# Four transfers made one, DRAM scratch laid out anew, and a reordered step in a delta-rule attention and ternary FFN kernel

## The chip, the cores and the metric

The kernel runs on one core of a Trainium2 chip. The metric is device time in microseconds (us) of one execution; lower is better. A profile comes from one execution of its own, and its span (first to last instruction) is a little shorter than that execution's time. The engines are PE (matrix multiply; PEld is its weight load), DVE (vector), ACT (scalar, activations), POOL (GpSimd) and SP, which here only issues DMA transfers.

## What is computed

Input x has 4 sequences of 4096 tokens of width 512, in float32. Two layers follow each other, each with a layer norm in front, one behind, and a residual.

```python
x = x + layernorm(attn(layernorm(x)))      # attn: a delta rule over time
x = x + layernorm(ffn(layernorm(x)))       # ffn: a ternary 512 x 512 weight

# attn, 16 heads of 32: rk = x normalised per head, wk = rk one step earlier,
# v = x @ Wv.T, gate and beta = sigmoid(x @ Wg.T), sigmoid(x @ Wb.T); per time step:
pred = einsum('bhk,bhkd->bhd', wk_t, S)
S    = S + wk_t[..., None] * ((v_t - pred) * b_t)[..., None, :]
o    = einsum('bhk,bhkd->bhd', rk_t, S) * g_t
# attn's result: o @ Wo.T

# ffn: layer norm with ln_gamma, ln_beta; w_q = clip(round(weight / (beta + EPS)), -1, 1)
# with beta = mean|weight|; xq = clip(xn * 128 / gamma) with gamma = max|xn| over everything;
# y = (xq @ w_q) * (gamma * beta / 128)
```

## The kernel before

Time is cut into 128 units of 32 tokens. A unit is 32 tokens of all four sequences, so its tiles have 128 partitions: partition `32*b + t` holds token t of sequence b. Within a unit the recurrence is solved as a block: a 32 x 32 triangular matrix per sequence and head is built, inverted, and applied to the right-hand side; only the small state S goes from one unit to the next.

Two strands of work run in one loop of steps.

- The strand of the blocks, at unit k ("AHEAD" in the plan): `load` brings x, `x_stats` and `x_norm` make its layer norm (DVE, then four small POOL instructions), `keys`, `keys_turn`, `key_squares`, `key_sums` and `key_norms` make the keys, `values` and `values_rest` multiply by Wv, `grams` multiplies keys by keys, `blocks` (ACT) and `masked` (POOL) turn that into the triangular blocks `nat`, which go to DRAM (`nat_d`). `hT` and `v` go to DRAM too (`hT_d`, `v_d`). `values` also makes `gr`, the gate moved by one token: two small transfers inside SBUF, one of 127 partitions (L248) and one of 4 partitions (L249); the second writes the same tile and waits on SP's queue until the first has landed.
- The inverses. `gather` reads `nat_d` back in another order, so that a partition holds one sequence and head (4 sequences x 32 heads of two units = 128) with a whole 32 x 32 block. `invert` works on groups of up to 8 units (DVE, `pr` L348 and `na` L354), a share of it at each place where the plan has a number such as 0.35. The inverses go to DRAM (`q_d`), and `fetch_inverse` reads them back with a token per partition.
- The strand of the chain, at unit i ("BACK"): `fetch` brings v and hT back, `again` brings x a second time for the residual, then `predict`, `apply`, `errors`, `outputs` and `grow` (the recurrence), `out_turn`, `project`, `residual` (with x1 to DRAM), `x1_stats`, `x1_norm`, `x1_turn`, `x1_scale`, `largest` (xn to DRAM), `ternary_a`, `ternary_b` and `finish`, which stores y.

Every transfer but a handful is issued by SP, in the order of the program. Each of `load`, `again`, `finish`, `gather` and `fetch_inverse` issues four transfers, one for each sequence b, with 32 partitions each.

The order of work on each engine is the order in which the functions are called: each instruction is tied to the one before it on its engine. The tuple `plan` is that order for a step with a unit of both strands or of the chain alone, `lead` the order for a step of the blocks alone. The first ten steps are `lead`. Then i counts from -2, k moves with it, and while k is less than i + 20 a further `lead` step comes in between: eight of them, for i = 0 to 7. From then on k = i + 20. So 108 steps (i = 0 to 107) have a unit of both strands. The steps from i = 108 on have no unit of the blocks left, and take `plan` without its AHEAD items. The last unit of the chain and the rest of the FFN stand in a list of their own behind the loop, then comes the global maximum, and a loop that repeats the few units in which the clip bites.

Of the kernel before, what the change touches and what calls it, by code (L numbers as in the profile page):

```python
# [8 lines left out]
F32 = mybir.dt.float32  # L9
# [4 lines left out]
P = 128  # L14
# [8 lines left out]
def kernel(  # L23
# [22 lines left out]
    nc = tc.nc  # L46
    B, T, D = x.shape
    H = wg.shape[0]
    DH = D // H
    KC = D // P  # L50
    NU = T // DH
# [5 lines left out]
    dram = ctx.enter_context(tc.tile_pool(name="dram", bufs=1, space=bass.MemoryType.DRAM))  # L57
# [3 lines left out]
    xn_d = dram.tile([NU, P, D], F32, name="xn_d")  # L61
    hT_d = dram.tile([NU, P, D], F32, name="hT_d")
    v_d = dram.tile([NU, P, D], F32, name="v_d")
    nat_d = dram.tile([NU // 2, P, 2 * H, DH], F32, name="nat_d")
    q_d = dram.tile([NU // 2, P, DH, DH], F32, name="q_d")

    def bank(name):
        return psum.tile([P, 512], F32, tag="bank", name=name)
# [21 lines left out]
    def quarters(b):  # L90
        return slice(b * DH, (b + 1) * DH)
# [18 lines left out]
    with ExitStack() as ph1:  # L110
# [7 lines left out]
        for b in range(B):  # L118
            s = quarters(b)
            nc.gpsimd.affine_select(  # L120
                out=mneg[s, :], in_=mneg[s, :], compare_op=ALU.is_gt, fill=0.0,
# [20 lines left out]
        firsts = [sum(sizes[:g]) for g in range(len(sizes))]  # L142
# [7 lines left out]
        def load(i):  # L150
            xt = wk.tile([P, D], F32, tag="x", name=f"x_{i}", bufs=4)
            cx[i]["x"] = xt
            for b in range(B):
                nc.sync.dma_start(out=xt[quarters(b), :], in_=x[b, i * DH : (i + 1) * DH, :])

        def x_stats(i):
            cx[i]["mv"] = mean_var(stat, cx[i]["x"], f"a{i}")
# [162 lines left out]
        def masked(i):  # L320
            nat = cx[i].pop("nat")
            masks(i).tensor_tensor(nat, nat, cx[i].pop("mb"), ALU.mult)  # L322
            w = i % 2 * H
            nc.sync.dma_start(out=nat_d[i // 2, :, w : w + H, :], in_=nat)

        nas = {}

        def gather(g, a):  # L330
            if a == 0:
                nas[g] = wk.tile([P, NP, DH, DH], F32, tag="na", name=f"na_{g}", bufs=2)
            for b in range(B):
                s = quarters(b)
                nc.sync.dma_start(
                    out=nas[g][s, a], in_=nat_d[firsts[g] // 2 + a, s].rearrange("s w t -> w s t")
                )

        def invert(g):

            np_ = sizes[g] // 2
            na = nas.pop(g)[:, :np_]

            def product(s, prs):
                m = DH - 1 - s
                pr = wk.tile([P, NP * (DH // 2) ** 2], F32, tag="pr", name=f"pr_{g}_{s}", bufs=1)
                prs[s] = pr[:, : np_ * m * s].rearrange("p (a n t) -> p a n t", a=np_, n=s)
                nc.vector.tensor_tensor(  # L348
                    prs[s], bcast(na[:, :, s, s + 1 :], [P, np_, s, m], 2),
                    bcast(na[:, :, :s, s], [P, np_, s, m], 3), ALU.mult,  # L350
                )

            def add(s, prs):
                nc.vector.tensor_tensor(  # L354
                    na[:, :, :s, s + 1 :], na[:, :, :s, s + 1 :], prs.pop(s), ALU.add
                )

            def ones():
                nc.vector.tensor_copy(
                    na.rearrange("p a t s -> p a (t s)")[:, :, :: DH + 1],  # L360
                    bcast(diag, [P, np_, DH], 1),
                )
                for a in range(np_):
                    nc.sync.dma_start(out=q_d[firsts[g] // 2 + a], in_=na[:, a])


            START = 190
            prs = {}
            ops = []
            for s in range(1, DH - 1):  # L370
                size = START + np_ * s * (DH - 1 - s)
                ops += [(size, product, (s, prs)), (size, add, (s, prs))]
            ops += [(START, ones, ())]
            whole = sum(o[0] for o in ops)
            for size, f, args in ops:
                f(*args)
                yield size / whole

        def fetch_inverse(i):
            if i % 2 == 0:  # L380
                q = wk.tile([P, 2, H, DH], F32, tag="q", name=f"q_{i}", bufs=2)
                for b in range(B):
                    s = quarters(b)
                    nc.sync.dma_start(
                        out=q[s].rearrange("p u h t -> p (u h) t"),
                        in_=q_d[i // 2, s].rearrange("w s t -> s w t"),
                    )
                cx[i]["q"], cx[i + 1]["q"] = q[:, 0], q[:, 1]

        inv = {"ops": None, "done": 0.0, "due": 0.0, "steps": 1}  # L390
# [102 lines left out]
        def again(i):  # L493
            xr = wk.tile([P, D], F32, tag="xr", name=f"xr_{i}", bufs=5)
            cx[i]["xr"] = xr
            for b in range(B):
                nc.sync.dma_start(out=xr[quarters(b), :], in_=x[b, i * DH : (i + 1) * DH, :])

        def turned(i, src, name):
            ps = bank(f"ps_{name}_{i}")  # L500
# [103 lines left out]
        def finish(i):  # L604
            my = cx[i]
            y = wk.tile([P, D], F32, tag="y", name=f"y_{i}")
            nc.vector.scalar_tensor_tensor(
                y, my.pop("ps_y"), my.pop("rs_y"), my.pop("x1"), op0=ALU.mult, op1=ALU.add
            )
            queue = nc.scalar if i > NU - 4 else nc.sync  # L610
            for b in range(B):
                queue.dma_start(out=out[b, i * DH : (i + 1) * DH, :], in_=y[quarters(b), :])


        raws = {}
# [62 lines left out]
        def ternary_centre():  # L678
# [13 lines left out]
        BACK, AHEAD = "chain's unit", "unit of the blocks"  # L692
        plan = (
            (AHEAD, 5, load), (BACK, 2, fetch), (BACK, 2, fetch_inverse), (BACK, 2, again),
            (BACK, 0, predict), (AHEAD, -1, blocks), (BACK, -1, out_turn), (BACK, -3, x1_turn),
            (BACK, 0, apply), (BACK, -3, x1_scale), (AHEAD, -1, masked),
            (AHEAD, 1, key_sums), (AHEAD, 3, x_stats), (AHEAD, 3, x_norm), (AHEAD, 1, key_norms),
            (AHEAD, 2, keys), (AHEAD, 2, key_squares), 0.2,
            (BACK, -4, ternary_a), (BACK, 0, errors), (BACK, -4, ternary_b), (BACK, 0, outputs),
            0.2, (BACK, 0, grow), (BACK, -2, x1_stats),  # L700
            (AHEAD, 2, keys_turn), (AHEAD, -1, gates), (BACK, 1, rekey), (BACK, 1, expand), (BACK, -4, finish),
            (BACK, -1, project), (BACK, -3, largest), 0.35, (BACK, -2, x1_norm),
            (BACK, -1, residual), (AHEAD, 0, values), (AHEAD, 0, values_out, half),
# [1 line left out]
            (AHEAD, 0, grams),  # L705
        )

        lead = (
            (AHEAD, 5, load), (AHEAD, 2, keys), (AHEAD, 3, x_stats),
            (AHEAD, 3, x_norm), (AHEAD, 0, values), (AHEAD, 1, key_sums), (AHEAD, 1, key_norms),  # L710
            (AHEAD, 2, key_squares), (AHEAD, -1, blocks), (AHEAD, 2, keys_turn),
            (AHEAD, -1, masked), 0.3,
            (AHEAD, 0, values_out, half), (AHEAD, 0, values_rest), (AHEAD, 0, writes), 0.35,
            (AHEAD, 0, values_out, 0), (AHEAD, -1, gates), (AHEAD, 0, grams), 0.35,
# [7 lines left out]
        k = START - 1  # L722
# [66 lines left out]
        for n, (i, k) in enumerate(steps):  # L789
            for g, (begin, end) in enumerate(spans):  # L790
                if begin == n:
                    inv.update(ops=invert(g), done=0.0, due=0.0, steps=end - begin)
            for ga in come.get(n, ()):
                gather(*ga)
            for item in lead if i is None else plan:
                if isinstance(item, float):
                    inverses(item)
                    continue
                base = i if item[0] == BACK else k
                if base is not None:  # L800
                    do(item[2], base + item[1], *item[3:])
            if any(end == n + 1 for _, end in spans):
                inverses(1.0)
            for f in between.get(n, ()):
                f()
            seen = in_order(seen)
# [20 lines left out]
        nc.vector.memset(both[:, 1:2], 1.0)  # L827
        N = NU - 1
        for f, i in (
            (predict, N), (out_turn, N - 1), (x1_turn, N - 3), (apply, N),  # L830
            (x1_scale, N - 3), (ternary_a, N - 4), (errors, N), (outputs, N), (ternary_b, N - 4),
            (x1_stats, N - 2), (project, N - 1), (x1_norm, N - 2), (largest, N - 3),
            (finish, N - 4), (out_turn, N), (x1_turn, N - 2), (x1_scale, N - 2), (project, N),
            (residual, N - 1), (x1_stats, N - 1), (x1_norm, N - 1), (largest, N - 2),
            (residual, N), (ternary_a, N - 3), (ternary_b, N - 3), (x1_stats, N), (x1_norm, N),
            (x1_turn, N - 1), (x1_scale, N - 1), (finish, N - 3), (ternary_a, N - 2),
            (ternary_b, N - 2), (largest, N - 1), (x1_turn, N), (x1_scale, N), (largest, N),
        ):
            do(f, i)
# [38 lines left out]
        for n in range(2):  # L878
            y = wk.tile([P, D], F32, tag="y", name=f"y_free{n}")
# [8 lines left out]
        with tc.For_i(0, count, 1) as n:  # L888
# [16 lines left out]
            y = wk.tile([P, D], F32, tag="e", name="y_again", bufs=1)  # L905
# [6 lines left out]
            for b in range(B):  # L912
                (nc.sync if b % 2 == 0 else nc.scalar).dma_start(
                    out=out[b, bass.ds(u * DH, DH), :], in_=y[quarters(b), :]
# [29 lines left out]
```

## Time and profile before

| | us |
|---|---|
| time before, median of three runs | 2457.53 (2445.64 to 2458.46) |
| the profiled execution | 2449.7, span 2448.0 |
| PE busy | 2260.7 (92%) |
| DVE busy | 2004.4 (82%) |
| ACT busy | 1738.8 (71%) |
| POOL busy | 1651.9 (67%) |
| queue of SP (q1): packets, MB, share of 16 DMA engines | 764368, 440.56, 70.2% |
| issues of x, xr (x again), out: each 64 KB | 512, 512, 500 and 12 on ACT's queue |
| issues of na from nat_d, and of q from q_d: each 128 KB | 256, 256 |
| issues of nat_d (256 KB), of q_d (512 KB) | 128, 64 |

The page gives busy time by engine, shares of 40 slices of the span, the DMA queues, the chain of work that ended last (walked back from the last instruction), and the costliest groups. A share of the DMA engines is a mean over 16 of them: 0.06 can be one engine that is busy all the time. Busy shares are also means over stages: up to 132 us there are steps of the blocks alone, from about 400 to 2090 us both strands run, behind that only the chain.

### The profile page before, as it was taken

The numbers are of one execution on the slowest core, as the hardware profiler recorded it, in microseconds if no ns is written. First come the engines' busy times: TensorE is split into PE (matmuls) and PEld (weight loads), VectorE is DVE, ScalarE is ACT, GpSimd is POOL, SyncE is SP. The second block draws the span as 40 slices with busy tenths as digits, with TensorE's granted clock in tenths as the row PEclk, the third lists the DMA queues.
The fourth block names the chain that finished last, engine by engine and source line by source line (L and its number), as shares of the span: only waits on it lengthen the run. The fifth ranks groups of instructions, "written<-read, shape, count | busy, mean of one in ns | idle before, by whom it ended". The sixth has DMA issues, their size and how long they took to land.

```text
span 2448.0 us, 61524 instructions
## 1 busy us (share of the span) xinstructions
PE 2260.7 (92%) x22563; PEld 1466.9 (60%) x22563; DVE 2004.4 (82%) x3058; ACT 1738.8 (71%) x3485; POOL 1651.9 (67%) x2701
## 2 busy tenths in 40 slices
PE   6678999899999999999999999999999999878896
PEld 5555666556666666666666666666666666444452
DVE  5887878888988888898988888898988888766652
ACT  5556777677777777777777777777777777545562
POOL 5977887777777777777777777777777776322221
PEclk8888999999999999999999999999999999989998
DMA  5577777777787878777778787777777777645442
GB/s 161 148 170 183 190 180 201 188 190 183 202 201 189 219 188 213 184 210 188 188 197 195 208 197 203 191 211 193 186 204 187 207 181 211 143 127 140 132 121 66
DMA packets 765341, 445.40 MB, mean 182 GB/s; under 512 B 591056, under 2 KB 591056, under 8 KB 765040
## 3 DMA queue, kind: packets, MB, share of 16 engines
q1 hardware_dynamic: 764368, 440.56, 70.2%
q8 instruction: 178, 2.92, 0.5%
q14 instruction: 123, 1.01, 0.2%
q10 hardware_dynamic: 672, 0.92, 0.1%
HBM read 205.07 MB, written 235.14 MB: 180 GB/s over the span
## 4 chain that ended last, share of the span: by engine, by line
PE 58%; DVE 9%; POOL 8%; DMA 8%; ACT 6%; issue 5%; SPq 5%; DVEq 0%; ACTq 0%; POOLq 0%
PE ps_y L586 16%; PE ps_wo L522 11%; PE ps_v L238 5%; PE ps_u L445 5%; PE ps_v L270 5%; PE ps_ds L481 4%; PE ps_gram L303 3%; PE ps_r L429 2%; POOL rn L218 2%; DMA gr<-gb 2%; ACT tbd L418 2%; PE ps_f L458 2%; PE ps_hT L183 2%; DVE na L354 2%; DVE r L435 2%
## 5 line engine op out<-in xcount | busy, mean ns | idle before, releaser
L586 PE MATMUL ps_y<-wq,xn 128*128 128x512 f32 x1024 | 512.9, 625 | 0.0
L348 DVE TENSOR_TENSOR pr<-na 128x336 f32<-128x336 f32 (+25 forms) x540 | 458.8, 850 | 17.7 <-DMA x<-in_L_attn_x_dram 6.0
L314 ACT COPY nat<-ps_gram 32x512 f32<-32x512 f32 x512 | 295.7, 578 | 240.3 <-PE ps_gram L303 235.7
L522 PE MATMUL ps_wo<-woT,oT 128*128 128x512 f32 x1024 | 463.4, 595 | 0.0
L354 DVE TENSOR_TENSOR na<-na,pr 128x336 f32<-128x336 f32 (+25 forms) x540 | 440.0, 815 | 7.5
L487 DVE TENSOR_TENSOR state<-ps_ds,state 32x512 f32<-32x512 f32 x508 | 348.7, 686 | 59.4 <-PE ps_ds L481 53.7
L218 POOL TENSOR_TENSOR rn<-ss,mhalf 128x16 f32<-128x16 f32 x128 | 387.5, 3027 | 10.7
L322 POOL TENSOR_TENSOR nat<-nat,mb 128x512 f32<-128x512 f32 x124 | 162.8, 1313 | 242.5 <-ACT nat L314 242.4
L418 ACT COPY tbd<-q 32x512 f32<-32x512 f32 x512 | 314.0, 613 | 6.9
L522 PEld LDWEIGHTS ps_wo<-woT,oT 128*128 128x128 f32 x1024 | 184.9, 191 | 187.0 <-issue 184.4
L238 PE MATMUL ps_v<-wvbT,hN 128*128 128x288 f32 x1024 | 279.5, 417 | 8.6 <-POOL hN L194 8.6
L586 PEld LDWEIGHTS ps_y<-wq,xn 128*128 128x128 f32 x1024 | 181.1, 197 | 159.5 <-issue 159.5
L238 PEld LDWEIGHTS ps_v<-wvbT,hN 128*128 128x128 f32 x1024 | 198.2, 195 | 105.2 <-issue 33.0
L270 PE MATMUL ps_v<-wvbT,hN 128*128 128x256 f32 x1024 | 243.9, 381 | 0.0
L445 PE MATMUL ps_u<-tbd,r 128*32 128x128 f32 x4096 | 146.5, 286 | 91.3 <-DVE r L435 88.2
L270 PEld LDWEIGHTS ps_v<-wvbT,hN 128*128 128x128 f32 x1024 | 194.9, 192 | 31.9
L461 DVE TENSOR_TENSOR e<-ps_f,bet 128x512 f32<-128x512 f32 x127 | 87.8, 692 | 149.5 <-PE ps_f L458 149.3
L568 ACT ACTIVATE xn<-ps_xn,lnb,lng 128x128 f32<-128x128 f32 x512 | 194.7, 469 | 0.3 <-PE ps_xn L502 0.3
L481 PEld LDWEIGHTS ps_ds<-e,h 32*128 32x128 f32 x4064 | 126.5, 188 | 101.0 <-DVE o L466 91.0
L531 DVE SCALAR_TENSOR_TENSOR x<-ps_wo,rstd_b,xr 128x512 f32<-128x512 f32 x128 | 96.0, 750 | 104.5 <-POOL rstd_b L95 101.6
L303 PE MATMUL ps_gram<-hT 32*128 32x128 f32 x4096 | 153.6, 287 | 29.6 <-ACT nat L314 29.6
L445 PEld LDWEIGHTS ps_u<-tbd,r 128*32 128x32 f32 x4096 | 110.2, 113 | 117.6 <-DVE r L435 79.2
(151 smaller groups left out, 3986.2 us busy)
## 6 DMA issues: line engine op xcount, KB each, us to landing
x<-in_L_attn_x_dram SPq DMA_DIRECT2D x512, 64.0 KB
hT_d<-hT SPq DMA_DIRECT2D x128, 256.0 KB
v_d<-v SPq DMA_DIRECT2D x128, 256.0 KB
nat_d<-nat SPq DMA_DIRECT2D x128, 256.0 KB
na<-nat_d SPq DMA_DIRECT2D x256, 128.0 KB
q_d<-na SPq DMA_DIRECT2D x64, 512.0 KB
v<-v_d SPq DMA_DIRECT2D x128, 256.0 KB
hT<-hT_d SPq DMA_DIRECT2D x128, 256.0 KB
```

Of the source, the lines that this page charges most:

```text
L218: nc.gpsimd.tensor_tensor(rn, ss, mhalf, ALU.pow)
L238: nc.tensor.matmul(ps[:, : half + 2 * H], lhsT=my["hN"][:, k, :], rhs=wvbT[:, k, half:], start=(k == 0), stop=(k == KC - 1),)
L270: nc.tensor.matmul(ps[:, :half], lhsT=my["hN"][:, k, :], rhs=wvbT[:, k, :half], start=(k == 0), stop=(k == KC - 1),)
L303: nc.tensor.matmul(ps[:, j, q * P : (q + 1) * P], lhsT=hT[rows, q, :], rhs=hT[rows, q, :], start=True, stop=True,)
L314: nc.scalar.copy(nat[s].rearrange("p (j q) t -> p j q t", j=HQ), ps[s].rearrange("p j (q t) -> p j q t", q=NQ)[:, :, :, s],)
L348: nc.vector.tensor_tensor(prs[s], bcast(na[:, :, s, s + 1 :], [P, np_, s, m], 2), bcast(na[:, :, :s, s], [P, np_, s, m], 3), ALU.mult,)
L354: nc.vector.tensor_tensor(na[:, :, :s, s + 1 :], na[:, :, :s, s + 1 :], prs.pop(s), ALU.add)
L418: nc.scalar.copy(tbds[i % NBD][s, :, s], q[s])
L445: nc.tensor.matmul(ps[quarters(j), qq * P : (qq + 1) * P], lhsT=r[:, hd * DH : (hd + 1) * DH], rhs=tbd[:, j * NQ + qq, :], start=True, sto ...
L487: nc.vector.tensor_tensor(S[s, :, :, s], psd[s].rearrange("p b (q d) -> p b q d", q=NQ)[:, :, :, s], S[s, :, :, s], ALU.add,)
L522: nc.tensor.matmul(ps, lhsT=oT[:, k, :], rhs=woT[:, k, :], start=(k == 0), stop=(k == KC - 1))
L586: nc.tensor.matmul(my["ps_y"], lhsT=my["xn"][:, k * P : (k + 1) * P], rhs=wq[:, k, :], start=(k == 0), stop=(k == KC - 1),)
```

## The change

Three kinds of edit:

1. One transfer for four. `load`, `again` and `finish` address all four sequences of x or out at once. `gather` and `fetch_inverse` do so too, for which `nat_d` and `q_d` have their dimensions in another order: in `nat_d` token, sequence, head, and in `q_d` head, sequence, token. So the reads are patterns of 128 rows at one distance; the writes into these arrays (`masked`, `ones` in `invert`), which went to 128 rows at one distance, now go to a pattern of 4 (sequences) x 32.
2. A tuple `late` of its own for steps whose k is over 128 (i from 109 on), and in the list behind the loop `residual` of unit N - 2 first, which `late` leaves to it.
3. `x_norm` (POOL) is called later, behind `outputs` in `plan` and behind `key_norms` in `lead`. In `lead` `blocks` comes earlier too.

```diff
-    nat_d = dram.tile([NU // 2, P, 2 * H, DH], F32, name="nat_d")
-    q_d = dram.tile([NU // 2, P, DH, DH], F32, name="q_d")
+    nat_d = dram.tile([NU // 2, DH, B, 2 * H, DH], F32, name="nat_d")
+    q_d = dram.tile([NU // 2, 2 * H, B, DH, DH], F32, name="q_d")
@@ load; again is the same with xr
-            for b in range(B):
-                nc.sync.dma_start(out=xt[quarters(b), :], in_=x[b, i * DH : (i + 1) * DH, :])
+            nc.sync.dma_start(out=xt, in_=x[:, i * DH : (i + 1) * DH, :])
@@ masked
-            nc.sync.dma_start(out=nat_d[i // 2, :, w : w + H, :], in_=nat)
+            nc.sync.dma_start(
+                out=nat_d[i // 2, :, :, w : w + H, :].rearrange("s b w t -> b s (w t)"),
+                in_=nat.rearrange("p w t -> p (w t)"),
+            )
@@ gather
-            for b in range(B):
-                s = quarters(b)
-                nc.sync.dma_start(
-                    out=nas[g][s, a], in_=nat_d[firsts[g] // 2 + a, s].rearrange("s w t -> w s t")
-                )
+            nc.sync.dma_start(
+                out=nas[g][:, a],
+                in_=nat_d[firsts[g] // 2 + a].rearrange("s b w t -> (b w) s t"),
+            )
@@ invert
-                    nc.sync.dma_start(out=q_d[firsts[g] // 2 + a], in_=na[:, a])
+                    nc.sync.dma_start(
+                        out=q_d[firsts[g] // 2 + a].rearrange("w b s t -> b w (s t)"),
+                        in_=na[:, a].rearrange("p s t -> p (s t)"),
+                    )
@@ fetch_inverse
-                for b in range(B):
-                    s = quarters(b)
-                    nc.sync.dma_start(
-                        out=q[s].rearrange("p u h t -> p (u h) t"),
-                        in_=q_d[i // 2, s].rearrange("w s t -> s w t"),
-                    )
+                nc.sync.dma_start(
+                    out=q.rearrange("p u h t -> p (u h) t"),
+                    in_=q_d[i // 2].rearrange("w b s t -> (b s) w t"),
+                )
@@ finish
-            for b in range(B):
-                queue.dma_start(out=out[b, i * DH : (i + 1) * DH, :], in_=y[quarters(b), :])
+            queue.dma_start(out=out[:, i * DH : (i + 1) * DH, :], in_=y)
@@ plan
-            (AHEAD, 1, key_sums), (AHEAD, 3, x_stats), (AHEAD, 3, x_norm), (AHEAD, 1, key_norms),
+            (AHEAD, 1, key_sums), (AHEAD, 3, x_stats), (AHEAD, 1, key_norms),
...
-            0.2, (BACK, 0, grow), (BACK, -2, x1_stats),
+            (AHEAD, 3, x_norm), 0.2, (BACK, 0, grow), (BACK, -2, x1_stats),
@@ new
+        late = (
+            (BACK, 2, fetch), (BACK, 2, fetch_inverse), (BACK, 2, again), (BACK, 0, predict),
+            (BACK, -2, residual), (BACK, -1, out_turn), (BACK, -3, x1_turn), (BACK, 1, rekey),
+            0.2, (BACK, 0, apply), (BACK, -3, x1_scale), (BACK, -4, ternary_a),
+            (BACK, -2, x1_stats), (BACK, 0, errors), (BACK, -4, ternary_b), (BACK, 0, outputs),
+            0.15, (BACK, 0, grow), (BACK, -2, x1_norm), (BACK, -4, finish), (BACK, 1, expand),
+            (BACK, -3, largest), (BACK, -1, project), 0.65,
+        )
@@ lead
-            (AHEAD, 5, load), (AHEAD, 2, keys), (AHEAD, 3, x_stats),
-            (AHEAD, 3, x_norm), (AHEAD, 0, values), (AHEAD, 1, key_sums), (AHEAD, 1, key_norms),
-            (AHEAD, 2, key_squares), (AHEAD, -1, blocks), (AHEAD, 2, keys_turn),
+            (AHEAD, 5, load), (AHEAD, -1, blocks), (AHEAD, 2, keys), (AHEAD, 3, x_stats),
+            (AHEAD, 0, values), (AHEAD, 1, key_sums), (AHEAD, 1, key_norms),
+            (AHEAD, 3, x_norm), (AHEAD, 2, key_squares), (AHEAD, 2, keys_turn),
@@ the loop
-            for item in lead if i is None else plan:
+            for item in lead if i is None else plan if k <= NU else late:
@@ the list behind the loop
-            (predict, N), (out_turn, N - 1), (x1_turn, N - 3), (apply, N),
+            (predict, N), (residual, N - 2), (out_turn, N - 1), (x1_turn, N - 3), (apply, N),
```

More of the change, by code (lines that the diff above doesn't have):

```diff
@@ L495, in again @@
             cx[i]["xr"] = xr
-            for b in range(B):
-                nc.sync.dma_start(out=xr[quarters(b), :], in_=x[b, i * DH : (i + 1) * DH, :])
+            nc.sync.dma_start(out=xr, in_=x[:, i * DH : (i + 1) * DH, :])
         def turned(i, src, name):
@@ L610, in finish @@
             queue = nc.scalar if i > NU - 4 else nc.sync
-            for b in range(B):
-                queue.dma_start(out=out[b, i * DH : (i + 1) * DH, :], in_=y[quarters(b), :])
+            queue.dma_start(out=out[:, i * DH : (i + 1) * DH, :], in_=y)
         raws = {}
```

## The prediction

> **What bounds the kernel now.** I read busy time by stage first: before both strands run, while they run (400 to 2090 us), the chain alone, and the end.
>
> ```profile
> 136.00:245.00 109.00, 87.99 (x942) 65.17 (x943) 87.25 (x151) 67.14 (x127) 82.50 (x131) 0.88 0.72 177
> 400.00:2090.00 1690.00, 1649.12 (x16964) 1077.17 (x16962) 1488.71 (x2200) 1295.40 (x2597) 1253.29 (x2015) 1.00 0.78 197
> 2090.00:2400.00 310.00, 261.20 (x2457) 144.16 (x2458) 195.92 (x305) 173.30 (x361) 82.05 (x164) 0.93 0.47 126
> 2400.00:2448.00 48.00, 27.95 (x65) 11.93 (x63) 10.07 (x25) 11.30 (x30) 6.77 (x21) 0.83 0.21 66
> ```
>
> Columns: stretch, length, busy us of PE, PEld, DVE, ACT, POOL, granted clock, DMA share, GB/s. In the long stage PE is busy 98% of the time: it is the bound, and the 16 DMA engines, at 0.78, are the next thing behind it. Outside, PE idles 146 us in all. The chain that ended last says the same: 58% PE, and SP's queue 5%.
>
> ```profile
> PE 58%; DVE 9%; POOL 8%; DMA 8%; ACT 6%; issue 5%; SPq 5%; DVEq 0%; ACTq 0%; POOLq 0%
> DMA packets 765341, 445.40 MB, mean 182 GB/s; under 512 B 591056, under 2 KB 591056, under 8 KB 765040
> q1 hardware_dynamic: 764368, 440.56, 70.2%
> ```
>
> The packet counts decide this case. Of the 591,056 packets under 512 B, gather and fetch_inverse make 512 x 1024 rows of 128 B = 524,288; gr 128 x (127 + 4) = 16,768; the two short vectors lng and lnb 1,024. 48,976 are left, and these are the 4-byte records that close a transfer. There are 3,277 transfers: at 16 records each, 52,432. The difference is 3,456 = 128 x 15 + 128 x 12. So a transfer has one record for each DMA engine that it uses: those of 128, 32 and 16 rows use sixteen, gr's 127-row transfer (L248) one, its 4-row transfer (L249) four. The second view of this is gr itself, on SP's queue and in the busy share just behind it:
>
> ```profile
> SPq L249 <- DMA gr<-gb: 252.3, 128, 3.1
> 1205.72 0.65 SPq L248 DMA_DIRECT2D gr<-gb  x1
> 1208.32 0.56 SPq L249 DMA_DIRECT2D gr<-gb  x1
> 1207.00:1208.00 1.00, 1.00 (x3) 0.33 (x2) 0.97 (x2) 1.00 (x4) 0.92 (x3) 1.00 0.09 8
> 1208.00:1209.00 1.00, 1.00 (x7) 0.74 (x6) 0.77 (x2) 1.00 (x2) 0.93 (x2) 1.00 0.00 0
> ```
>
> SP waits about 2 us in every unit for 8 KB; in that time one engine of 16 works (0.09), then none. By the packet records the 127 rows start 7 ns apart, 0.89 us in all, and the median time from the last of them to the next large packet is 1.87 us. Today that hole is idle DMA time that nobody needs.
>
> **The change part by part: the transfers.** x and out are addressed as 4 sequences x 32 tokens x 512, with 8 MB between sequences, so the four can't merge into one count of 128; the tile's side is 128 rows. The writes into nat_d and q_d become 4 x 32 too. The reads of gather and fetch_inverse do merge to 128 rows. The trace has no transfer with 4 on one side and 128 on the other. The bounds are sixteen engines (every transfer with 128 rows) and four (gr's 4-row one). I take four: the outermost count of DRAM is the same 4 as in gr, and a split by whole outer rows can't give sixteen engines a share each.
>
> The Trainium skill ("DMA: Bandwidth & Descriptors", section "Why a DMA increments its semaphore by 16 and not by 1") speaks against the change here: the number of engines is the largest up to 16 that divides the slowest dimension of both patterns, and on SP's kind of queue they are the lowest-numbered ones. The record count agrees for 127, 4, 32 and 16 rows. By this rule the sum is the one below; if only the tile's rows counted, it would be rival A's.
>
> Four engines then carry all of load, again, finish, masked and ones, and their sixteenth of all else. Durations are medians of packet records: 2 KB 84 ns (mean 102), 4 KB 159 (mean 170). Packets of 128 B overlap on an engine, so I take their rate: 1,400 a microsecond over 16 engines, 11.4 ns each. (Means times counts give 68.5% of 16 spans for the three sizes, of the 70.2% above.) The work of the busiest engine, per unit with both strands:
>
> - four transfers of 256 KB (x, x again, out, nat), 32 packets of 2 KB each: 4 x 32 x 84 ns = 10.75 us. Over sixteen engines they took 2.69.
> - q_d, half a transfer of 512 KB: 32 packets of 4 KB per pair, 2.54 us.
> - hT_d, v_d, v, hT, x1, xn over sixteen: 6 x 8 x 84 ns = 4.03 us.
> - 128-byte rows, 256 of them: 2.92 us.
> - gr 0.89 us, closing records 0.12 us.
>
> Sum 21.25 us. The unit takes 17.1 us now ((2090 - 136 - 107) / 108, with 107 us for the eight extra lead steps), so this engine becomes the bound. To it comes the hole around gr: behind L249 on SP's queue stand v_d and all transfers of the next step, so nothing is issued until the 127 rows have landed, and these stand behind everything issued before. If gr's engine is one of the four, they drain in each unit: 1.87 us. The same once a group, where fetch_inverse waits for q_d: 1.87 / 8 = 0.23. That is 23.35 us per unit, times 108 = 2522 us.
>
> A lead step has load, nat, q_d, hT_d, v_d, gather and gr: 5.38 + 2.54 + 1.34 + 1.46 + 0.89 + 0.10 + 2.10 = 13.8 us; eight of them 110 us. The twelve steps before the first `predict` took 131.8 us; with 23 us of start and somewhat slower steps (q_d is hardly there yet) I take 155. The chain alone needs again and out 5.38, four over sixteen engines 2.69, 128-byte rows 1.46: 9.5 us per step against some 16, so DMA isn't its bound, and it stays at 358 us with the end. Sum: 2522 + 110 + 155 + 358 = 3145 us of span, 1.7 us more for the execution (2449.7 against 2448.0): 3147. The median of the runs shown is 0.3% above the profiled one, inside the error of the sum.
>
> Bounds: the best microseconds of the trace (199 packets of 2 KB, 104 of 4 KB, 1,600 of 128 B over 16 engines: 80, 154 and 10 ns) give 20.2 us without any hole, and 2710 us with the tail at its least; with a hole of 1.55 us 2895. Mean packet durations (102, 170, 16 ns) give 26.4 + 2.1 us per unit and 3760 us.
>
> **SP's issues.** Per unit 9 of load, again and finish go and 3 of gather and fetch_inverse, at a median of 0.42 us: 12 x 0.42 = 5 us less on SP's queue, of the 25.6 issues per unit. SP is 5% of the chain, 122 us; 47% of its issues gone is worth up to 57 us. In the forecast it is worth nothing, as SP waits for the DMA engines instead; in rival A it is the gain.
>
> **The order of late steps.** `late` moves whole functions, with the transfers of x1, xn and out on SP's queue in the new order; residual's x1 comes a step later, and x1_stats of the same unit stands behind it in the same step. The tail's PE idle time (310 - 261 = 49 us) bounds a gain; a loss is bounded by one more chain of residual, x1_stats (ACT, then POOL) and x1_norm per step, some 3 us by the waits of vpe_b and x (2 to 3 us each at the longest) x 18 steps = 54. I take 0: both ends are equally near.
>
> **x_norm later.** Four POOL instructions (0.83, 0.57, 0.23, 0.19 us: 1.8 us a unit) move behind `outputs` on POOL; no transfer moves with them. `keys` of that unit comes a step later, so a whole step covers them. Now they hold POOL up for x's statistics (65 us in all, wait of vpe_a on mv_a), and with them `outputs`, which feeds the next step's out_turn. POOL is busy 74% of the long stage with PE at 98%: between 0 and the 41 us that PE idles there, 0 taken, as PE doesn't wait for POOL in any large row. Without the cover 1.8 us a unit would be 195 us, but nothing late waits for it. `blocks` earlier in `lead` moves ACT's copies in at most 20 steps; 0, within the 47 us that PE idles before 136 us.
>
> **The rivals.** A: sixteen engines are used all the same. For it: every 128-row transfer of the trace has sixteen records. Against: none of these has 4 on its other side. Then PE stays the bound and SP's 57 us come off: 2393 us, faster; from 2261 (PE's busy time) to 2450. The change then does what it says. B: four engines, but not the same ones each time. Then no engine is over-full (70% of 16 in the mean), a 256 KB transfer takes 2.7 us instead of 0.7, gr waits about 2 us longer on SP, which the 5 us saved cover: about 2440 us. Against it: nothing in the trace tells engines apart, but gr's fixed counts of one and four show a fixed split. C: four engines, with each packet slower, as all four sequences are read in step. The mean packet is 102 ns against 84, so some are slow today; with 130 ns for the 128 packets the unit grows by 5.9 us: 3780 us.
>
> Of this distance the skill says in the same page ("Latency and other measured facts") that rows 4 or 8 MiB apart halved the rate of large copies, and no run here shows it.
>
> **How the numbers follow.** Forecast 0.80, A 0.10, B 0.04, C 0.06. The time is the forecast's, 3147. The range 2780 to 3660 leaves out A and B (0.14), C, and little of the forecast at either end; the forecast's own range is the same. Differences under 0.5% can't be told from none. Faster: A 0.08 and B 0.01; same: 0.03; slower: the rest, 0.88.
>
> **What would show it.** After the change there are 1,741 transfers: 576 of the five changed kinds on four engines, 256 of gr, 909 on sixteen. Packets under 512 B should be 524,288 + 16,768 + 1,024 + 14,544 + 2,304 + 640 = 559,568; with sixteen engines 566,480. The mean DMA share should fall to about 0.55, though DMA is the bound, and the rate to 142 GB/s; PE's busy share to some 72%, with waits for x, xr, v or q that are absent now; SP's wait for gr should grow from 2 us to most of a step. Wrong it would be with 566,480, or with 559,568 and a time near 2450 (B).

## The result and the profile after

| | before | after |
|---|---|---|
| median | 2456.22 us (2445.64 to 2458.46, 4 runs) | 3437.64 us (3433.92 to 3439.47, 4 runs) |
| ratio | | 1.4006 (95% interval 1.3963 to 1.4048) |
| span of the profiled execution | 2448.0 us | 3437.1 us |

The change makes the kernel 40% slower. The page of the changed kernel, first busy time by engine, then the packet counts, the queue and the chain that ended last:

```profile
PE 2473.5 (72%) x22563; PEld 1586.1 (46%) x22563; DVE 2016.3 (59%) x3058; ACT 1731.8 (50%) x3485; POOL 1610.4 (47%) x2701
...
DMA packets 733836, 445.14 MB, mean 130 GB/s; under 512 B 559568, under 2 KB 559568, under 8 KB 733552
...
q1 hardware_dynamic: 733060, 440.43, 51.6%
...
DMA 39%; PE 18%; SPq 13%; DVE 13%; issue 7%; POOL 6%; ACT 3%; DVEq 0%; POOLq 0%; ACTq 0%
```

None of PE, DVE, ACT and POOL is a bound any more, and the mean over the DMA engines has fallen from 70% to 52%: nothing looks full. The count in the second line says why that mean misleads. 559,568 is the number that the prediction gave for four engines in each changed transfer; sixteen would have left 566,480. The stretch by microseconds, around gr in the changed kernel, shows the four at work (columns as before: stretch, length, PE, PEld, DVE, ACT, POOL, clock, DMA share, GB/s):

```profile
1531.00:1532.00 1.00, 1.00 (x6) 0.83 (x5) 0.65 (x1) 0.87 (x3) 0.00 (x0) 1.00 0.26 100
1533.00:1534.00 1.00, 1.00 (x33) 0.91 (x32) 0.00 (x0) 0.00 (x0) 0.00 (x0) 1.00 0.00 0
1535.00:1536.00 1.00, 0.28 (x12) 0.01 (x2) 0.00 (x0) 0.99 (x2) 0.78 (x3) 1.00 0.70 252
1550.00:1551.00 1.00, 1.00 (x3) 0.38 (x2) 0.99 (x2) 1.00 (x3) 0.85 (x3) 1.00 0.26 102
1551.00:1552.00 1.00, 1.00 (x4) 0.49 (x3) 0.95 (x3) 0.99 (x3) 0.78 (x3) 1.00 0.26 102
```

A share of 0.26 is four engines of sixteen, full. The line of 1533 is the hole behind gr: nothing moves. In the line of 1535 the spread transfers run; by 1550 they are done, and the four go on alone to the end of the unit. By the packet records, mean of units 30 to 117, more than five packets are under way in 10.7 us of a unit, four or five in 11.5, one to three in 1.9, and none in 1.95. SP's queue in the same unit, its list of issues in order of time:

```profile
1524.35 0.68 SPq L248 DMA_DIRECT2D gr<-gb  x1
1533.34 0.57 SPq L249 DMA_DIRECT2D gr<-gb  x1
...
1536.10 1.14 SPq L387 DMA_DIRECT2D q<-q_d  x1
1537.29 6.57 SPq L499 DMA_DIRECT2D xr<-in_L_attn_x_dram  x1
```

gr stands behind all that was issued before it and lands after 9 us here; SP waits 8.2 us for it in the mean instead of 2 (1045.7 us over 128 units, 252.3 before). On the engines the waits follow from that: gr is multiplied on POOL, and rstd_b, which releases the residual on DVE, is queued there behind it.

```profile
POOL gr L294 <- DMA gr<-gb: 872.7, 114, 32.7
DVE x L533 <- POOL rstd_b L96: 785.8, 110, 29.6
PEld ps_oT L504 <- DVE x L533: 426.1, 81, 16.7
ACT h L170 <- DMA xr<-in_L_attn_x_dram: 421.8, 47, 26.4
```

By gr's packet records in units 30 to 117, a unit takes 26.0 us in the mean (17.6 before); by place in a group of eight it is 22.0, 26.3, 22.0, 24.3, 22.0, 24.1, 22.0 and 45.4. The last is the unit in which four inverses go to q_d. In 1.95 us of 26.0 no packet is under way (1.92 of 17.6 before).

### The profile page after: what moved, and what is told of

Same layout as the page of the kernel before. It is cut to its first block, busy times and chain, and to the rows that moved or that the text cites. A ratio compares the mean times of both kernels' runs of the same rounds, so it can differ in the third digit from the quotient of the medians.

```text
span 3437.1 us, 59282 instructions
## 1 busy us (share of the span) xinstructions
PE 2473.5 (72%) x22563; PEld 1586.1 (46%) x22563; DVE 2016.3 (59%) x3058; ACT 1731.8 (50%) x3485; POOL 1610.4 (47%) x2701
## 2 busy tenths in 40 slices
DMA packets 733836, 445.14 MB, mean 130 GB/s; under 512 B 559568, under 2 KB 559568, under 8 KB 733552
## 3 DMA queue, kind: packets, MB, share of 16 engines
q8 instruction: 178, 2.92, 0.4%
## 4 chain that ended last, share of the span: by engine, by line
DMA 39%; PE 18%; SPq 13%; DVE 13%; issue 7%; POOL 6%; ACT 3%; DVEq 0%; POOLq 0%; ACTq 0%
DMA gr<-gb 32%; PE ps_y L588 8%; SPq L499 5%; PE ps_u L448 4%; DVE na L356 3%; DVE pr L350 2%; DMA xr<-in_L_attn_x_dram 2%; DVE v L258 2%; DVE r L438 2%; DMA q_d<-na 2%; PE ps_wo L524 2%; SPq L580 2%; POOL rstd_b L96 2%; DMA x<-in_L_attn_x_dram 2%; SPq L410 1%
## 5 line engine op out<-in xcount | busy, mean ns | idle before, releaser
L588 PE MATMUL ps_y<-wq,xn 128*128 128x512 f32 x1024 | 593.0, 710 | 0.0
L294 POOL TENSOR_TENSOR gr<-gr,rn 128x16 f32<-128x16 f32 x128 | 32.6, 255 | 872.7 <-DMA gr<-gb 872.7
L504 PE MATMUL ps_oT<-ident,o 128*128 128x128 f32 x512 | 103.9, 337 | 404.0 <-DVE x L533 401.9
L218 POOL TENSOR_TENSOR rn<-ss,mhalf 128x16 f32<-128x16 f32 x128 | 381.3, 2979 | 10.7
L448 PE MATMUL ps_u<-tbd,r 128*32 128x128 f32 x4096 | 199.2, 356 | 243.2 <-DVE r L438 243.2
L170 ACT ACTIVATE h<-xr,nba,rsa 128x512 f32<-128x512 f32 x128 | 104.8, 819 | 422.1 <-DMA xr<-in_L_attn_x_dram 421.8
L588 PEld LDWEIGHTS ps_y<-wq,xn 128*128 128x128 f32 x1024 | 208.7, 226 | 201.1 <-issue 200.7
L238 PEld LDWEIGHTS ps_v<-wvbT,hN 128*128 128x128 f32 x1024 | 204.3, 201 | 160.6 <-POOL hN L194 62.6
L448 PEld LDWEIGHTS ps_u<-tbd,r 128*32 128x32 f32 x4096 | 145.1, 142 | 287.7 <-DVE r L438 222.0
L504 PEld LDWEIGHTS ps_oT<-ident,o 128*128 128x128 f32 x512 | 66.3, 166 | 437.6 <-DVE x L533 426.1
L454 ACT COPY ft<-ps_u 128x512 f32<-128x512 f32 x128 | 74.8, 584 | 377.9 <-PE ps_u L448 377.5
```

What stands on the lines that cost most here:

```text
L218: nc.gpsimd.tensor_tensor(rn, ss, mhalf, ALU.pow)
L238: nc.tensor.matmul(ps[:, : half + 2 * H], lhsT=my["hN"][:, k, :], rhs=wvbT[:, k, half:], start=(k == 0), stop=(k == KC - 1),)
L448: nc.tensor.matmul(ps[quarters(j), qq * P : (qq + 1) * P], lhsT=r[:, hd * DH : (hd + 1) * DH], rhs=tbd[:, j * NQ + qq, :], start=True, sto ...
L588: nc.tensor.matmul(my["ps_y"], lhsT=my["xn"][:, k * P : (k + 1) * P], rhs=wq[:, k, :], start=(k == 0), stop=(k == KC - 1),)
```

## The experiments

Every kernel's ratio is against runs of the kernel before on the same chip, with its 95% interval.

**1 and 2: orders alone, transfers alone.** The first is the changed kernel with the transfers of before, the second the kernel before with the changed transfers and layouts.

```diff
@@ orders alone, against the changed kernel: load, and so on for the other transfers and layouts
-            nc.sync.dma_start(out=xt, in_=x[:, i * DH : (i + 1) * DH, :])
+            for b in range(B):
+                nc.sync.dma_start(out=xt[quarters(b), :], in_=x[b, i * DH : (i + 1) * DH, :])
...
@@ transfers alone, against the changed kernel: plan, lead, late and the list as before
-            for item in lead if i is None else plan if k <= NU else late:
+            for item in lead if i is None else plan:
...
```

> The changed kernel with all transfers as before (four for one, nat_d and q_d in the old layout), so that only the new orders are left: late, the later x_norm, the other lead. Theory (four engines bound it): the orders cost or bring nothing large, 2430 to 2480 us. Rival (the reordered steps cause part of the loss): over 2510 us.

> The kernel before with the five changed transfers and the two layouts alone, orders as before. Theory: 3400 to 3480 us, within 1.5% of the changed kernel. Rival (the reordered steps cause part of the loss): under 3350 us.

Measured: orders alone 2440.69 us, ratio 0.9952 (0.9929 to 0.9974); transfers alone 3444.34 us, 1.405 (1.399 to 1.411). The loss is the transfers' and nothing else's.

**3: transfers without a kernel.** This kernel only moves data (one run): N = 48 units in each of six ways, then 128 stores to out.

```python
nc.sync.dma_start(out=t[quarters(b), :], in_=x[b, units(i), :])            # four for a unit
nc.sync.dma_start(out=t, in_=x[:, units(i), :])                            # one
nc.sync.dma_start(out=t[b * DH : (b + 2) * DH, :], in_=x[b : b + 2, units(i), :])   # two
nc.sync.dma_start(out=near[i, :, :DH, :], in_=t)    # near: [NU, 4, 33, 512], 66 KB apart
nc.sync.dma_start(out=t, in_=near[i, :, :DH, :])
nc.sync.dma_start(out=flat[i], in_=t)               # 128 rows at one distance
nc.sync.dma_start(out=out[:, units(i), :], in_=t)
```

> Transfers alone, no computation (the output is one tile of x in all places). In this order 48 units each: x by four transfers, by one (pattern 4 x 32, 8 MB apart), by two (2 x 32); one store and one load with a pattern of 4 x 32 that is 66 KB apart; one store of 128 rows at one distance; then 128 stores to out by one (4 x 32, 8 MB). Theory: one transfer of 4 x 32 runs at four engines, 2.69 us each (95 to 100 GB/s), at both distances; two run at two engines, 5.4 us per unit (48 GB/s); 128 rows at 0.67 us (over 350 GB/s); x by four limited by SP's issue, 1.7 us a unit. Rival C (8 MB apart makes packets slow): far ones below 70 GB/s, near ones at 97. Sixteen engines: all at 350 GB/s or at SP's issue.

The stretches in that order; the last two columns are DMA share and GB/s:

```profile
20.00:90.00 70.00, 0.00 (x0) 1.00 0.48 141
110.00:210.00 100.00, 0.00 (x0) 1.00 0.26 102
240.00:460.00 220.00, 0.00 (x0) 1.00 0.13 51
480.00:580.00 100.00, 0.00 (x0) 1.00 0.26 102
600.00:700.00 100.00, 0.00 (x0) 1.00 0.26 102
725.00:755.00 30.00, 0.00 (x0) 1.00 0.86 321
780.00:1060.00 280.00, 0.00 (x0) 1.00 0.26 102
```

One transfer of 4 x 32 rows goes at 102 GB/s, two of 2 x 32 at 51: half as many engines, half the rate, though twice as many transfers. A transfer of 128 rows at one distance reaches 321 over a stretch that holds some of its neighbours too. The rate stays at 102 with several transfers queued (behind the last load SP waits 11.1 us, the time of some four), so each takes the same four; rotating engines (rival B) would have overlapped them. Loads and stores 8 MB apart and 66 KB apart go at one rate: rival C is out. The rule of the Trainium skill in "DMA: Bandwidth & Descriptors", "Why a DMA increments its semaphore by 16 and not by 1", that the number of engines is the largest up to 16 that divides the slowest dimension of both sides, holds here for 4 against 128 and for 2 against 64.

**4 to 6: parts of the transfers.** In the kernel before, load alone as one transfer; load, again and finish; the two layouts with their reads and writes.

```diff
@@ load alone, against the kernel before
-            for b in range(B):
-                nc.sync.dma_start(out=xt[quarters(b), :], in_=x[b, i * DH : (i + 1) * DH, :])
+            nc.sync.dma_start(out=xt, in_=x[:, i * DH : (i + 1) * DH, :])
@@ three: the same for again and finish
...
@@ scratch: the hunks of nat_d, q_d, masked, gather, invert and fetch_inverse of the change
...
```

> The kernel before with load alone as one transfer. Busiest engine per unit: 2.69 + 9 x 0.67 + 0.64 + 2.92 + 1.01 = 13.3 us, with the hole 15.2, under the 17.1 us of a unit. Theory of throughput: no change, 2435 to 2475 us, though 128 transfers are on four engines. Rival (a transfer's longer landing time itself costs, whatever the sum): 2 us a unit, over 2650 us.

> The kernel before with load, again and finish as one transfer each; gather, fetch_inverse and the layouts as before. Busiest engine per unit: 8.06 (three on four engines) + 4.70 (seven on sixteen) + 0.64 (q_d) + 2.92 + 0.89 + 0.12 = 17.3 us, with the hole of 1.87 us 19.2 against 17.1 us now: +230 us, about 2690 us. If the excess of the changed kernel over the prediction (2.4 us a unit) comes with it: up to 2950. If sixteen engines were used or the engines rotated: 2400 to 2450 us.

> The kernel before with the new layouts of nat_d and q_d alone (masked and ones on four engines, gather and fetch_inverse one transfer); load, again, finish as before. Mean work of the busiest engine 2.69 + 2.54 + 9 x 0.67 + 2.92 + 1.01 = 15.2 us a unit, with holes 17.3, about the 17.1 of a unit. Theory of mean throughput: 2450 to 2500 us. Rival (the 20 us of a group's q_d writes come in one step and can't be spread): each of some 14 groups loses 14 to 20 us, 2650 to 2740 us.

Measured: 2696.86 us, 1.100 (1.0962 to 1.1039); 2972.2 us, 1.2124 (1.2072 to 1.2176); 2982.87 us, 1.217 (1.212 to 1.2221). All three are slower than the theory gave. load alone, which should have cost nothing, costs 10%, as its rival had it (over 2650 us); the three x transfers come near the 2950 us that the changed kernel's excess would give; the layouts lie above theory and rival. So the kernel before had less room than the expectations took. The first view of the prediction hints at it: a DMA share of 0.78 of 17.1 us is 13.3 us per engine, where a sum by medians gives 11.3 (ten transfers over sixteen engines 6.72, q_d 0.64, 128-byte rows 2.92, gr and records 1.01). With gr's 0.9 us and the hole of 1.9 us, 16.1 of 17.1 us were taken. From that base each transfer of 256 KB that goes from sixteen engines to four adds 24 x 84 ns = 2.02 us, and q_d 1.9:

| | sum | measured, mean unit |
|---|---|---|
| load | 18.1 us | 19.7 us |
| load, again, finish | 22.2 | 22.3 |
| nat_d, q_d | 20.0 | 22.1 |
| all five | 26.1 | 26.0 |

Where the engine is far over PE's 17.1 us the sum comes within 0.1 us. That is closer than it can claim. It was made after these results; with the 17.6 us that gr's records give for a unit before, it is 0.4 us higher; and the share counts packets of 128 B twice where they overlap on an engine, by the prediction's figures up to 256 x (16 - 11.4) ns = 1.2 us a unit. This microsecond of the kernel before has a share over 1:

```profile
1211.00:1212.00 1.00, 1.00 (x21) 0.88 (x18) 0.75 (x2) 0.89 (x3) 1.00 (x1) 1.00 1.19 185
```

The two cases near 17.1 cost 1.6 and 2.1 us more than the sum. In the scratch case part of this is the rival's burst: its last unit of a group takes 40.7 us, the others 18 to 22.

**7 to 9: without SP's wait for gr.** gr's second transfer writes one row that the first doesn't touch, so that SP goes on at once; what it leaves out are rows 32, 64 and 96. This is tried in the changed kernel, in the kernel before, and in the one with load as one transfer.

```diff
-                out=gr[::DH, :], in_=first[(0 if i == 0 else DH - 1) :: DH, :]
+                out=gr[0:1, :], in_=first[(0 if i == 0 else DH - 1) : (1 if i == 0 else DH), :]
```

> The changed kernel with gr's second transfer writing row 0 alone, so that it no longer overlaps the first and SP doesn't wait for gr (the gates of rows 32, 64 and 96 are left wrong by this). Theory (four engines busy all the time outside the hole): the hole of 1.87 us a unit goes, some 200 us less, 3200 to 3270 us. Rival (a loop: gr's landing, POOL, DVE, PE, SP's next issue, so that the engines idle within it too): over 350 us less, down to the sum without holes, 2920 us.

> The kernel before with the same edit of gr's second transfer (the gates of rows 32, 64 and 96 are left wrong by this). Both theories: PE is the bound, SP's 252 us of waiting cost nothing: 2435 to 2460 us. Under 2420 us would say that SP's queue mattered before.

> The kernel before with load as one transfer, and gr's second transfer writing row 0 alone, so that SP doesn't wait for gr (the gates of rows 32, 64 and 96 are left wrong by this). Theory (time is the busiest engine's work, with the DMA share of the long stage for the base: 0.78 x 17.1 = 13.3 us, + 0.9 for gr + 2.0 for load on four engines = 16.2 us, and the hole gone): under PE's 17.1 us again, 2440 to 2490 us. Rival (a long landing time costs by itself, through the eight transfers that SP may have open): over 2600 us, since load lands no sooner.

Measured: 3252.77 us, 1.3272 (1.3219 to 1.3325), 185 us less than the changed kernel; 2441.79 us, 0.9963 (0.9948 to 0.9977); 2540.18 us, 1.036 (1.0338 to 1.0383). In the changed kernel the time without any packet falls from 1.95 to 0.48 us per unit and the unit from 26.0 to 24.5 us, while the time with packets under way stays at 24.1 us: what goes is the hole, as the theory has it, and a loop through POOL and PE, the rival's cause, isn't needed to explain it. The same hole cost the kernel before only 0.4%, where PE, busy 98% of its long stage, was the bound. With load as one transfer it is worth 157 of some 250 us, and the time left lies between theory and rival; the other 90 us are over what the sum of 16.2 us allows. They go with a full SP queue, for which the record shows two things. The first is waits for transfers to land. Each of SP's transfers waits until the eighth before it has landed (the program counts them on eight semaphores in turn); with load as one, hT_d is the eighth behind it. SP's waits in the kernel with load as one:

```profile
SPq L248 <- DMA gr<-gb: 311.0, 128, 7.1
SPq L187 <- DMA x<-in_L_attn_x_dram: 179.2, 52, 4.4
```

The second line has no counterpart in the kernel before. The second thing is the issue of q, here in the kernel with load as one (3.29 us in the kernel before, shown in experiment 10):

```profile
1226.60 7.58 SPq L383 DMA_DIRECT2D q<-q_d  x4
```

With load as one and gr apart, SP's issues of x in the middle three fifths of the span take 59 us in place of 184, but those of q 318 in place of 134. With its waits SP is taken for some 98% of the time there, so the merged load gave its queue no room. Which of the two things costs the 90 us wasn't tried by itself; for load as one the DMA engine's sum alone isn't shown to be the cause.

**10: the new layouts, written in four.** gather and fetch_inverse stay one transfer of 128 rows, the writes go back to sixteen engines.

```diff
-            nc.sync.dma_start(
-                out=nat_d[i // 2, :, :, w : w + H, :].rearrange("s b w t -> b s (w t)"),
-                in_=nat.rearrange("p w t -> p (w t)"),
-            )
+            for b in range(B):
+                nc.sync.dma_start(
+                    out=nat_d[i // 2, :, b, w : w + H, :].rearrange("s w t -> s (w t)"),
+                    in_=nat[quarters(b)].rearrange("p w t -> p (w t)"),
+                )
@@ ones: the same for q_d
...
```

> The kernel before with the new layouts of nat_d and q_d and with gather and fetch_inverse as one transfer of 128 rows each, but masked and ones write in four transfers of 32 rows. Theory (the loss of the scratch arrays is that of their writes on four engines): 2435 to 2475 us, as before. Rival (the reads at a distance of 16 KB in the new layouts, or one long read in place of four, cost it): over 2600 us.

Measured: 2656.18 us, 1.0833 (1.0808 to 1.0858). Of the 533 us that the layouts cost, 328 were their writes on four engines; 205 stay, against the theory, and the rival's 2600 us are passed. Slow rows, the first half of the rival, don't explain it: a transfer of 4096 rows of 128 B, from first to last row, takes 3.46 us (median) where the four together took 3.71. The sums point to SP's issues. First two lines of the kernel before, then two of this one:

```profile
1234.20 3.29 SPq L384 DMA_DIRECT2D q<-q_d  x4
1237.54 2.23 SPq L497 DMA_DIRECT2D xr<-in_L_attn_x_dram  x4
```

```profile
1201.82 0.43 SPq L389 DMA_DIRECT2D q<-q_d  x1
1202.30 4.78 SPq L502 DMA_DIRECT2D xr<-in_L_attn_x_dram  x4
```

The one read is issued in 0.43 us, but the four behind it then take 4.78 in place of 2.23: 5.2 us for both, 5.5 before. So one read for four saves SP next to nothing, while four writes for one cost it more. In the middle three fifths of SP's issues they add up to 1152 us of 1466 in the kernel before, and 1269 of 1589 here (the writes into nat_d go from 36 us to 147, those into q_d from 33 to 78; x, xr, gather and fetch_inverse together go from 593 to 577). With gr's wait (some 164 us in each) and 50 ns between two issues SP is taken for about 97% of the time in both. SP's queue was as full as PE before, though some 250 of its 1152 us lie above the median issue of 0.42 us, in issues that were held. The 117 us more stand beside a stretch that is 123 us longer; an edit that relieves SP alone, which would show the cause, wasn't tried.

**11 and 12: the orders apart.** late alone; x_norm later and the new lead alone.

```diff
@@ late alone, against the kernel before, with the tuple late and the list's residual
-            for item in lead if i is None else plan:
+            for item in lead if i is None else plan if k <= NU else late:
...
@@ the other, against the kernel before, with the new lead
-            (AHEAD, 1, key_sums), (AHEAD, 3, x_stats), (AHEAD, 3, x_norm), (AHEAD, 1, key_norms),
+            (AHEAD, 1, key_sums), (AHEAD, 3, x_stats), (AHEAD, 1, key_norms),
...
-            0.2, (BACK, 0, grow), (BACK, -2, x1_stats),
+            (AHEAD, 3, x_norm), 0.2, (BACK, 0, grow), (BACK, -2, x1_stats),
...
```

> The kernel before with the tuple late for steps from i = 109 on, and residual of N - 2 first behind the loop, alone. All orders together brought 0.5% (10 to 12 us). If late brings it: 2430 to 2440 us, with PE's busy share up in the stretch from 2090 us. If x_norm and lead bring it: within 0.2% of before.

> The kernel before with x_norm later in plan and the new lead alone. If late brings the 0.5% of all orders: within 0.2% of before. If these do: 2430 to 2440 us, with a shorter stretch before the first predict.

Measured: late alone 2426.95 us, 0.9906 (0.9878 to 0.9933); the other two 2461.82 us, 1.0046 (1.0028 to 1.0063). late alone beats both kernels. Up to the last gr both run alike (2089.9 us, 2090.8 before); the gain lies behind it. The waits of the chain's last stretch, 2090 or 2100 to 2400 us, first of the kernel before, then with late:

```profile
POOL vpe_y L601 <- ACT junk_y L508: 169.5, 19, 12.1
ACT ft L451 <- PE ps_u L445: 75.2, 19, 6.8
```

```profile
POOL vpe_y L601 <- ACT junk_y L508: 45.1, 23, 10.7
ACT ft L451 <- PE ps_u L445: 43.7, 20, 4.8
```

ACT waits 31 us less for PE's ps_u in the recurrence; POOL's wait moves to vpe_c and is no measure. The loss by x_norm and lead is 0.5%. Its first predict comes at 139.0 us (131.8 before), not sooner as expected; but the profiled execution, the fastest of its nine, shows no loss at its end (2450.5 us), so the cause stays open.

## Why the prediction was right, and where its size was off

- **Four engines, always the same:** right, to the last packet record, and shown at 102 GB/s without a kernel around it. Rivals A, B and C are out.
- **The work of the busiest engine, 21.25 us a unit:** the mechanism was right, the term too small. It is 24.07 us (26.02 less 1.95 without packets, if the busiest engine works whenever a packet is under way), 2.8 us more, times 108 units some 300 us; the misses elsewhere are small. The step that was off is "Durations are medians of packet records". The changed kernel's mean 2 KB packet takes 104.8 ns, and 80 of them per unit and engine by 20.8 ns make 1.7 us; 4096 rows of 128 B take 3.68 us in place of 2.92, 0.8 us (3.71 already in the kernel before); 4 KB packets of 179 ns in place of 159 make 0.3 us. The 80 are a mean over sixteen engines; the busiest one carries 176, and that it has only an equal part of the excess is assumed. Alone, four engines keep 84 ns (experiment 3); in the changed kernel a 2 KB packet takes 89 ns in the mean while at most four packets are under way, and 112 ns while nine or more are, so the excess lies mostly where spread transfers run beside them. The upper bound by mean durations, 26.4 us, was 2.3 us too high.
- **The hole around gr, 1.87 + 0.23 us:** 1.95 us measured, and 185 us gone with it where 200 were expected.
- **The group's q_d writes, 20.4 + 1.9 us in the unit that has them:** 45.4 us against 22.0 to 24.3 in most others, so 21 to 23.
- **The ends:** 155 us to the first predict became 174, and the 358 us from the last gr on became 365. The chain alone isn't bound by DMA, as said.
- **SP's issues, worth nothing in the forecast:** right for the changed kernel, where SP waits for the engines. But "47% of its issues gone is worth up to 57 us" rested on a count of issues; by the issue times of experiment 10 a merged read of short rows gives its time to the next issue.
- **late, 0 between -49 and +54 us:** about -23 us. **x_norm and lead, 0 with a gain of up to 41 and 47 us:** about +11 us, outside the gain that was allowed. Beside 980 us neither decides.
- **What would show it:** a DMA share of 0.52 over the span (0.55 forecast), 130 GB/s (142), SP's wait for gr 8.2 us a unit, a third of it rather than most. PE at 72%, as forecast, is luck: its busy time rose from 2261 to 2473 us; without that, 3437 us would have given 66%.

## What to carry to other kernels

Before four transfers become one, write down the outermost count of both sides' patterns as the instruction will have them: 4 against 128 rows ran on four engines at 102 GB/s, where four transfers of 32 rows ran on sixteen. A mean share over the engines hides it; the number of closing records under 512 B and a share that stands at 0.26 show it. And check a sum of packet medians against the busy share of the stage it describes: here 11.3 against 13.3 us, of which up to 1.2 is overlap, said beforehand that the medians were low. Add up the issuing queue too, its issues and its waits: fewer issues gave SP no room here.

## What the hardware showed that was not expected

An issue on SP's queue can carry the time of the one before it: 0.4 us for a transfer of 4096 short rows, then 4.8 us for four short ones behind it. PE's granted clock fell to 0.84 in the changed kernel's long stage (1.00 before), and the mean matmul of ps_y rose from 625 to 710 ns, while that of ps_wo stayed (595 and 597); whether this cost time wasn't tried. The Trainium skill ("DMA: Bandwidth & Descriptors", "Latency and other measured facts") has the rate of copies between DRAM tensors halved where 128 rows lie 4 or 8 MiB apart; with four sequences 8 MB apart no loss shows here: 102 GB/s, as at 66 KB.
